# Cross attention: router weights made the stationary operand in four column groups, with a new order of the steps

## The chip, the cores and the metric

The kernel runs on one core of one Trainium2 chip. The metric is the device time of the whole program in microseconds (us), as the median of repeated executions. Four executions of the kernel before took 3863.5, 3868.45, 3855.14 and 3864.93 us; their median is 3864.22 us.

The engines are named as in the profile: PE is the matrix engine (PEld its weight loads), DVE the vector engine, ACT the scalar engine, POOL the GpSimd engine, SP the queue that issues most transfers. PE multiplies a stationary operand, which is loaded into the array first, by a moving operand that streams past it. Results land in PSUM, and another engine has to read them out.

## The reference

The model is one decoder layer in float32 on 32 sequences of 128 tokens with 512 features: differential self attention, cross attention, and a mixture of experts. Cut to what matters here:

```
x = x + self_attention(layernorm(x))
x = x + cross_attention(layernorm(x), ctx)      # 128 channels (the tokens), 8 heads of 16, 512 positions
h = layernorm(x).reshape(4096, 512)
scores = sigmoid(h @ gate_w)                    # gate_w: 512 x 32, the router
# best 2 of 4 groups of experts, then the best 6 experts of those; weights normalized
out = x + experts(h, chosen, weights) + shared_expert(h)
```

The change is about `h @ gate_w`, which is computed for each sequence (128 tokens x 512 features times 512 x 32), and about the order in which all the work of cross attention and of the routing is issued.

## The kernel before

The program has five stages that follow each other: self attention, cross attention with the routing, the first three groups of the shared expert, the routed experts, and the last five groups of the shared expert. The change lies in the second one, `CrossAttention`, and in the few calls to it that run at the end of the first and at the start of the third.

**Steps.** Cross attention handles one sequence ("batch" b) at a time and pipelines them. A batch has 16 steps, two sides of the heads by four chunks of 128 queries by two pairs of heads; batch b begins at step 16 b. In step n, `maxima` (L685) multiplies queries by keys in two row groups of the array (L691) and DVE takes the negated maximum of each row (L695, tile `nm`). Eleven steps later `exponentials` (L708) multiplies the same operands the other way round, with the maxima folded in (L714), and ACT takes the exponential (L718, tile `xp`). The two products of one step use opposite pairs of row groups, so they can run side by side. `weigh` (L721) sums values by these weights for a whole side at once: 16 products in four column groups of 32 (L729), after which DVE transposes the result (L736, tile `xu`).

**Order.** `plan` (L798) lists every other piece of work of a batch with a step, counted from 16 b, and a phase. `advance` (L847) runs through the steps: in each it issues the pieces with phase `first` or `sooner`, then the exponentials, then `middle`, then the maxima, then `after` and `later`. That loop stands under a manual schedule, so PE, DVE, ACT and POOL execute in exactly the order in which the pieces are issued; only SP's queue is ordered by the framework. Since batches overlap, what matters in the steady state is the step modulo 16. We write r0 to r15 for it.

**PSUM.** `Common.banks` (L46) hands out PSUM in turn from four buffers. Each product of any piece takes one; the fifth taker waits until the reader of the first is done. A step takes two.

**The other pieces** and what they issue: `project` (L644; PE L648, ACT L650, POOL L651), `rotate` (L654; DVE L658, four POOL instructions), `measure` and `measure_out` (two ACT passes L73 and L74, three small POOL ones), `normalize` and `normalize_out` (ACT L87), `values` (PE L678, two ACT copies L680), `turn_maxima` (PE L96, DVE L703), `divide` (DVE L746, POOL L748), `turn_out` (DVE L756), `leave` (PE L765, ACT L769, POOL L770, a store), `hand_over` (stores, PE L96, ACT L786), `router` (PE L793, ACT L946, POOL L947), and of the routing `sigmoid` (DVE), `groups` (DVE, POOL), `choose` (DVE, POOL), `take` (DVE L999 and L1004), `count` (PE L1011 and L1012, DVE, POOL L1016), `slots_of` (DVE L1022, POOL) and six times `enter` (POOL, an indirect transfer, L1028).

A float32 product runs as two passes, so a product shows as two records of PE and two weight loads.

Of the kernel before, what the change touches and what calls it, by code (L numbers as in the profile page):

```python
# [10 lines left out]
F32 = mybir.dt.float32  # L11
I32 = mybir.dt.int32
AF = mybir.ActivationFunctionType
ALU = mybir.AluOpType
AX = mybir.AxisListType
# [3 lines left out]
P = 128  # L19
E = 512  # L20
EC = E // P
# [4 lines left out]
NX = 32  # L26
# [73 lines left out]
class Later:  # L100
# [5 lines left out]
    def put(self, step, phase, call, *args):  # L106
        self.calls.append(((step, phase), call, args))
# [420 lines left out]
class CrossAttention:  # L528
# [49 lines left out]
    def prepare(self, heads):  # L578
        nc, wp = self.nc, self.wp
        TC, NH, C = self.TC, self.NH, self.C  # L580

        self.keep = wp.tile([P, 2], F32, name="keep")
        nc.vector.tensor_reduce(self.keep, heads.rearrange("p (j s) -> p s j", s=2), AX.X, ALU.add)
        lane = wp.tile([P, 1], I32, name="lane")
        nc.gpsimd.iota(lane, pattern=[[0, 1]], base=0, channel_multiplier=1)
        nc.vector.tensor_scalar(lane, lane, 31, None, ALU.bitwise_and)
        self.extra = wp.tile([P, 2], F32, name="extra")
        for side in range(2):
            nc.vector.tensor_scalar(
                self.extra[:, side : side + 1], lane, float(self.ROW[side]), None, ALU.is_equal  # L590
            )
        self.zero = wp.tile([P, 1], F32, name="zero")
        nc.vector.memset(self.zero, 0.0)

        self.nm = [[wp.tile([P, TC, P], F32, name=f"nm{s}{i}") for i in range(2)] for s in range(2)]
        self.v2 = [wp.tile([P, TC, NH, 2 * C], F32, name=f"v2{i}") for i in range(2)]
        for t in (*self.nm[0], *self.nm[1]):  # L600
            nc.gpsimd.memset(t, 0.0)
        for t in self.v2:
            nc.gpsimd.memset(t, 1.0)


        self.wT = {}
        for n in "qkvo":
            ps = self.cm.banks()[:, 0, 0:P]
            nc.tensor.transpose(ps, self.nat[n], self.cm.ident)
            self.wT[n] = wp.tile([P, P], F32, name=f"{n}T")  # L610
            nc.vector.tensor_copy(self.wT[n], ps)


        one = wp.tile([P, 1], F32, name="x_one")
        nc.vector.memset(one, 1.0)
        ps = self.cm.banks()[:, 0, 0:1]
        nc.tensor.matmul(ps, self.rotT, one, start=True, stop=True)
        sign = wp.tile([P, 1], F32, name="sign")
        nc.vector.tensor_copy(sign, ps)
        nc.vector.tensor_scalar(self.sin["k"], self.sin["k"], sign, None, ALU.mult)  # L620
        for t, name in ((self.cos, "cosq"), (self.sin, "sinq")):
            t["q"] = wp.tile([P, E], F32, name=name)
            nc.vector.tensor_scalar(t["q"], t["k"], 0.25, None, ALU.mult)


        ps = self.cm.banks()[:, 0, 0:1]
        nc.tensor.matmul(ps, self.wT["o"], self.bv, start=True, stop=True)
        nc.vector.tensor_tensor(self.bo, self.bo, ps, ALU.add)
# [157 lines left out]
        self.nc.scalar.copy(self.out[b], tr)  # L786
        self.nc.sync.dma_start(out=self.h3T_d[b], in_=self.out[b])

    def router(self, b):
        h3T = self.out.pop(b)  # L790
        pl = self.cm.banks()[:, 0, 0:NX]
        for c in range(EC):
            self.nc.tensor.matmul(  # L793
                pl, h3T[:, c, :], self.gw[:, c, :], start=c == 0, stop=c == EC - 1
            )
        self.routing.scores(b, pl)

    def plan(self, load_shared, load_tokens):  # L798

        S, put, routing = self.S, self.todo.put, self.routing  # L800
        first, sooner, middle, after, later = self.PHASES
        for b in range(self.B):
            at = 2 * S * b
            put(at - 20, sooner, self.load, b)
            put(at - 16, sooner, self.project, b, "k")
            put(at - 12, sooner, self.measure, b)
            put(at - 9, sooner, self.rotate, b, "k")
            put(at - 10, sooner, self.normalize, b)
            put(at - 9, sooner, self.project, b, "q")
            put(at - 6, middle, self.rotate, b, "q")  # L810
            put(at + 2, sooner, self.values, b)
            put(at + 9, later, self.turn_maxima, b, 0)
            put(at + 17, later, self.turn_maxima, b, 1)
            put(at + 10, sooner, self.load_again, b)
            put(at + 29, later, self.divide, b)
            put(at + 34, later, self.turn_out, b)
            put(at + 38, later, self.leave, b)
            put(at + 43, later, self.measure_out, b)
            put(at + 48, sooner, self.normalize_out, b)
            put(at + 50, sooner, self.hand_over, b)  # L820
            put(at + 58, sooner, self.router, b)
            put(at + 59, sooner, routing.sigmoid, b)
            put(at + 63, middle, routing.groups, b)
            put(at + 66, middle, routing.choose, b)
            put(at + 66, later, routing.take, b)
            put(at + 70, later, routing.count, b)
            put(at + 80, sooner, routing.slots_of, b)
            for k in range(TOPK):
                put(at + 82 + 5 * k // 2, later, routing.enter, b, k)
            put(at + 19, after, self.weigh, b, 0, 0)  # L830
            put(at + 20, first, self.weigh, b, 0, 1)
            put(at + 28, after, self.weigh, b, 1, 0)
            put(at + 28, later, self.weigh, b, 1, 1)
        put(20, later, load_shared)
        put(2 * S * (self.B - 2), later, load_tokens)
        self.todo.calls.sort(key=lambda x: x[0])
        self.steps = [
            (b, side, c, pair)
            for b in range(self.B) for side in range(2) for c in range(self.TC) for pair in range(2)
        ]  # L840
# [869 lines left out]
```

## Time and profile before

| What | Value |
|---|---|
| Median of four executions | 3864.22 us |
| The profiled execution's own time | 3864.3 us |
| Its span | 3862.6 us, 1.7 us less than its time |
| PE busy | 3776.2 us (98%) |
| DVE, ACT, POOL busy | 53%, 43%, 61% |
| Granted PE clock, mean | 0.993 |
| Cross attention, 798 to 1797 us, PE busy | 971.82 of 999.00 us |
| From one router product to the next in the steady state | 33.05 us (27 times, within 0.01) |

The busy share of PE must be read with care. A record of a product covers its way through the array, and the records of row or column groups that run side by side overlap. PE counts as busy as long as any record is open, also where the next product could have begun earlier. So 98% does not say that PE could not go faster. How long a stretch of work takes is read from the starts of its records, not from the busy share.

### The profile page before, as it was taken

What the parts mean: (1) busy time and instruction counts of PE and PEld (TensorE: products, weight loads), DVE (VectorE), ACT (ScalarE), POOL (GpSimd) and SP (SyncE); (2) the same over time, 40 slices, a digit from 0 to 9 for tenths busy, and PEclk for the clock granted to TensorE, in tenths of its full rate; (3) what the DMA queues carried; (4) which work ended last, traced back from release to release, by engine and by line L of the source; (5) the groups of instructions that cost most, each with busy time, mean ns of one, the idle gap of its engine ahead of it and who ended that gap; (6) DMA issues with size and microseconds to landing.
All of it is one profiled execution on the core that took longest, in us unless ns stands there. A gap on an engine that the chain in (4) does not pass through costs nothing. (4 is left out here: it accounts for less than half of the span.)

```text
span 3862.6 us, 58185 instructions
## 1 busy us (share of the span) xinstructions
PE 3776.2 (98%) x19060; PEld 2010.3 (52%) x19060; DVE 2057.6 (53%) x3202; ACT 1678.3 (43%) x4032; POOL 2349.2 (61%) x2582
## 2 busy tenths in 40 slices
PE   8999999899999999999999999999999999999999
PEld 5666666434444444444445555555555555555444
DVE  5888888777778778777223333333333333333111
ACT  6989998857776777676201111111111111111000
POOL 3545554645777777776337777777777777775000
PEclk9999999899999999999999999999999999999999
DMA  3111110121111111111156777676767777776210
GB/s 111 34 34 37 37 36 26 39 83 50 61 61 50 50 48 47 50 50 34 60 160 165 173 170 169 162 176 153 183 153 166 169 185 154 173 168 155 87 57 33
DMA packets 285988, 387.21 MB, mean 100 GB/s; under 512 B 147889, under 2 KB 179249, under 8 KB 285617
## 3 DMA queue, kind: packets, MB, share of 16 engines
q0 software_dynamic: 62912, 109.85, 15.9%
q1 hardware_dynamic: 81792, 190.98, 15.2%
q10 hardware_dynamic: 140976, 82.60, 7.7%
q8 instruction: 154, 2.52, 0.3%
q14 instruction: 154, 1.25, 0.1%
HBM read 617.52 MB, written 143.07 MB: 197 GB/s over the span
## 5 line engine op out<-in xcount | busy, mean ns | idle before, releaser
L1422 POOL DMA_INDIRECT e_xr<-h_d,e_run_of x832 | 849.1, 1020 | 281.3 <-issue 269.6
L695 DVE TENSOR_REDUCE nm<-ps 128x2 f32<-128x1024 f32 x512 | 610.7, 1215 | 112.4 <-PE ps L691 105.5
L718 ACT ACTIVATE xp<-ps 128x1024 f32<-128x1024 f32 x512 | 505.8, 1021 | 264.9 <-PE ps L691 200.7
L1452 DVE TENSOR_TENSOR e_gu<-e_act,ps 128x352 f32<-128x352 f32 x208 | 108.4, 521 | 942.1 <-ACT e_act L1451 568.3
L1483 PE MATMUL ps<-wd,e_guT 128*128 128x512 f32 (+1 forms) x1248 | 572.8, 595 | 11.3 <-DMA wd<-in_L_ffn_w_down_dram 5.2
L714 PE MATMUL ps<-xqn,xk 32*128 32x512 f32 x2048 | 527.1, 620 | 20.5 <-ACT xp L718 19.1
L1447 PE MATMUL ps<-wg,e_xT 128*128 128x352 f32 x1664 | 528.9, 460 | 4.0 <-DMA wg<-in_L_ffn_w_gate_dram 4.0
L691 PE MATMUL ps<-xk,xq 32*128 32x512 f32 x2048 | 527.4, 630 | 0.5 <-DVE nm L695 0.4
L1447 PE MATMUL ps<-wu,e_xT 128*128 128x352 f32 x1664 | 526.5, 459 | 0.4 <-DMA wu<-in_L_ffn_w_up_dram 0.3
L1451 ACT ACTIVATE e_act<-ps 128x352 f32<-128x352 f32 x208 | 96.3, 463 | 923.1 <-PE ps L1447 426.4
L1447 PEld LDWEIGHTS ps<-wg,e_xT 128*128 128x128 f32 x1664 | 315.3, 190 | 238.9 <-issue 104.3
L1488 POOL DMA_INDIRECT sum_d<-e_y,e_into x208 | 335.9, 1615 | 130.8 <-issue 79.8
L1447 PEld LDWEIGHTS ps<-wu,e_xT 128*128 128x128 f32 x1664 | 316.0, 190 | 177.8 <-DMA wu<-in_L_ffn_w_up_dram 1.5
L279 ACT ACTIVATE s<-s,a_nm 128x128 f32<-128x128 f32 x1024 | 395.5, 394 | 5.3 <-DVE a_nm L265 4.5
L1483 PEld LDWEIGHTS ps<-wd,e_guT 128*128 128x128 f32 (+1 forms) x1248 | 236.6, 191 | 261.2 <-issue 219.3
L714 PEld LDWEIGHTS ps<-xqn,xk 32*128 32x128 f32 x2048 | 168.6, 183 | 284.1 <-ACT xp L718 123.2
L1487 ACT ACTIVATE e_y<-ps,e_weight 128x512 f32<-128x512 f32 x208 | 142.9, 687 | 395.8 <-PE ps L1483 268.6
L1473 DVE STREAM_TRANSPOSE e_guT<-e_gr 96x384 f32<-96x384 f32 (+1 forms) x416 | 230.9, 555 | 60.4 <-DMA e_gr<-e_gu_d 46.1
L228 POOL TENSOR_SCALAR k<-kz,a_keep,a_extra 128x256 f32<-128x256 f32 x128 | 82.4, 653 | 285.9 <-ACT kz L227 285.9
L1028 POOL DMA_INDIRECT table_d<-entry,at x192 | 202.3, 1054 | 64.2 <-issue 53.3
L729 PE MATMUL ps<-xp,v 128*32 128x512 f32 x2048 | 233.0, 595 | 7.9 <-ACT xp L718 7.6
L1434 DVE STREAM_TRANSPOSE e_xT<-e_xr 128x512 f32<-128x512 f32 x208 | 226.4, 1089 | 8.1 <-DMA e_xr<-h_d,e_run_of 8.0
(272 smaller groups left out, 5275.7 us busy)
## 6 DMA issues: line engine op xcount, KB each, us to landing
wg<-in_L_ffn_w_gate_dram SPq DMA_DIRECT2D x208, 704.0 KB
wu<-in_L_ffn_w_up_dram SPq DMA_DIRECT2D x208, 704.0 KB
wd<-in_L_ffn_w_down_dram SPq DMA_DIRECT2D x208, 576.0 KB
e_gu_d<-e_gu ACTq DMA_DIRECT2D x208, 192.0 KB
e_gr<-e_gu_d ACTq DMA_DIRECT2D x208, 192.0 KB
wd<-in_L_ffn_w_down_dram SPq DMA_DIRECT2D x208, 128.0 KB
e_xr<-h_d,e_run_of POOLq DMA_INDIRECT x832
xres<-in_x_dram SPq DMA_DIRECT2D x32, 256.0 KB
```

What stands on the lines that cost most here:

```text
L279: nc.scalar.activation(s[:, j, c, side, :], s[:, j, c, side, :], AF.Exp, bias=nm[n][:, side, at : at + 1], accum_out=sm[n][:, to : to + 1],)
L691: self.nc.tensor.matmul(sc[:, i, :], q[rows, ts(c, P)], k[rows, :], start=True, stop=True)
L695: self.nc.vector.tensor_reduce(at[:, self.ROW[side], 2 * pair : 2 * pair + 2], sc, AX.X, ALU.max, negate=True)
L714: self.nc.tensor.matmul(sc[:, i, :], k[rows, ts(c, P)], q[rows, :], start=True, stop=True)
L718: self.nc.scalar.activation(e, sc, AF.Exp)
L729: self.nc.tensor.matmul(po[b, side][ts(j, 32), :], self.v2[b % 2][:, c, 2 * j + side, :], es[j // 2][:, j % 2, :], start=c == 0, stop=c == ...
L1422: self.cm.nc.gpsimd.indirect_dma_start(out=xr[:, t, :], out_offset=None, in_=self.h3_d.rearrange("t (q f) -> (t q) f", q=self.Q), in_offse ...
L1434: self.cm.nc.vector.transpose(xT.rearrange("p c (t i) -> p c t i", t=self.Q), self.xr.pop(i).rearrange("p t (j c) -> p c t j", c=EC),)
L1447: nc.tensor.matmul(pgu[:, half, 0:M], t[:, c, :], w[:, c, :], start=c == 0, stop=c == EC - 1)
L1473: self.cm.nc.vector.transpose(t[rows, 0:n, :].rearrange("p c (t i) -> p c t i", t=self.Q), g[rows, :, 0 : 32 * n].rearrange("p t (j c) -> ...
L1483: nc.tensor.matmul(py, t[:n, c, :], self.wd[s][:n, c, :], start=c == 0, stop=c == len(M_CHUNKS) - 1)
L1488: nc.gpsimd.indirect_dma_start(out=self.sum_d[:, :], out_offset=bass.IndirectOffsetOnAxis(ap=self.into[:, i : i + 1], axis=0), in_=y[:, :] ...
```

## The change

In `prepare`, a new tile `x_stack` (128 x 32) is made once: four 32 x 32 identities on top of each other. The router is split in two pieces. `logits` multiplies in four column groups: chunk c of the router weights (128 x 32) is the stationary operand of column group c, and the transposed tokens of the same chunk (128 x 128) stream past it. The four partial sums land in 32 rows each of one 128 x 128 PSUM area, and ACT copies that to SBUF (`x_parts`). `router` then multiplies `x_parts` as stationary operand by `x_stack`, which adds the four parts and turns them back to tokens by experts.

All steps and phases in `plan` are new. In the order in which they now come in a period: `hand_over` at r0; `turn_maxima` of side 1 and `values` at r1; `project` k and `measure` at r2; `choose`, `turn_out`, `rotate` k, `take`, `logits` and `normalize` at r3; `weigh` of side 0 at the turn from r3 to r4; `count` at r5; `leave` at r6; `router`, `turn_maxima` of side 0, `project` q, `slots_of`, `measure_out` and `rotate` q at r10; `sigmoid`, `groups` and `normalize_out` at r11; `weigh` of side 1 at the turn from r11 to r12; `load` and `divide` at r14.

```diff
+        self.stack = wp.tile([P, NX], F32, name="x_stack")
+        nc.vector.tensor_reduce(
+            self.stack, self.cm.ident.rearrange("p (c e) -> p e c", e=NX), AX.X, ALU.add
+        )
...
-    def router(self, b):
+    def logits(self, b):
+
         h3T = self.out.pop(b)
-        pl = self.cm.banks()[:, 0, 0:NX]
+        parts = self.cm.banks()[:, 0, 0:P]
         for c in range(EC):
             self.nc.tensor.matmul(
-                pl, h3T[:, c, :], self.gw[:, c, :], start=c == 0, stop=c == EC - 1
-            )
+                parts[ts(c, NX), :], self.gw[:, c, :], h3T[:, c, :], start=True, stop=True
+            )
+        self.out[b] = self.p2.tile([P, P], F32, name="x_parts")
+        self.nc.scalar.copy(self.out[b], parts)
+
+    def router(self, b):
+        pl = self.cm.banks()[:, 0, 0:NX]
+        self.nc.tensor.matmul(pl, self.out.pop(b), self.stack, start=True, stop=True)
         self.routing.scores(b, pl)
...
-            put(at - 20, sooner, self.load, b)
-            put(at - 16, sooner, self.project, b, "k")
-            put(at - 12, sooner, self.measure, b)
-            put(at - 9, sooner, self.rotate, b, "k")
-            put(at - 10, sooner, self.normalize, b)
-            put(at - 9, sooner, self.project, b, "q")
-            put(at - 6, middle, self.rotate, b, "q")
-            put(at + 2, sooner, self.values, b)
-            put(at + 9, later, self.turn_maxima, b, 0)
+            put(at - 18, middle, self.load, b)
+            put(at - 14, sooner, self.project, b, "k")
+            put(at - 14, middle, self.measure, b)
+            put(at - 13, middle, self.rotate, b, "k")
+            put(at - 13, later, self.normalize, b)
+            put(at - 6, sooner, self.project, b, "q")
+            put(at - 6, later, self.rotate, b, "q")
+            put(at + 1, later, self.values, b)
+            put(at + 10, sooner, self.turn_maxima, b, 0)
             put(at + 17, later, self.turn_maxima, b, 1)
-            put(at + 10, sooner, self.load_again, b)
-            put(at + 29, later, self.divide, b)
-            put(at + 34, later, self.turn_out, b)
-            put(at + 38, later, self.leave, b)
-            put(at + 43, later, self.measure_out, b)
-            put(at + 48, sooner, self.normalize_out, b)
-            put(at + 50, sooner, self.hand_over, b)
+            put(at + 26, later, self.load_again, b)
+            put(at + 30, later, self.divide, b)
+            put(at + 35, middle, self.turn_out, b)
+            put(at + 38, sooner, self.leave, b)
+            put(at + 42, later, self.measure_out, b)
+            put(at + 43, later, self.normalize_out, b)
+            put(at + 48, sooner, self.hand_over, b)
+            put(at + 51, later, self.logits, b)
             put(at + 58, sooner, self.router, b)
-            put(at + 59, sooner, routing.sigmoid, b)
-            put(at + 63, middle, routing.groups, b)
-            put(at + 66, middle, routing.choose, b)
-            put(at + 66, later, routing.take, b)
-            put(at + 70, later, routing.count, b)
-            put(at + 80, sooner, routing.slots_of, b)
+            put(at + 59, later, routing.sigmoid, b)
+            put(at + 59, later, routing.groups, b)
+            put(at + 67, middle, routing.choose, b)
+            put(at + 67, later, routing.take, b)
+            put(at + 69, later, routing.count, b)
+            put(at + 74, later, routing.slots_of, b)
             for k in range(TOPK):
-                put(at + 82 + 5 * k // 2, later, routing.enter, b, k)
-            put(at + 19, after, self.weigh, b, 0, 0)
-            put(at + 20, first, self.weigh, b, 0, 1)
-            put(at + 28, after, self.weigh, b, 1, 0)
-            put(at + 28, later, self.weigh, b, 1, 1)
+                put(at + 81 + 5 * k // 2, later, routing.enter, b, k)
+            put(at + 19, later, self.weigh, b, 0, 0)
+            put(at + 20, sooner, self.weigh, b, 0, 1)
+            put(at + 27, later, self.weigh, b, 1, 0)
+            put(at + 28, sooner, self.weigh, b, 1, 1)
```

## The prediction

> **What bounds the kernel now.** I read the page's engine table first, then the stretches by stage, then the chain that ended last, then PE's timeline over one period of cross attention, and last the groups.
>
> ```profile
> PE 3776.2 (98%) x19060; PEld 2010.3 (52%) x19060; DVE 2057.6 (53%) x3202; ACT 1678.3 (43%) x4032; POOL 2349.2 (61%) x2582
> ...
> by line: PE ps L1215 4.5%; PE ps L1247 2.2%; PE ps L1231 0.4%; PE ps L1254 0.3%; DVE s_x L1258 0.0%; issue 0.0%
> ...
> 1208.77:1241.82 33.05, 32.18 (x234) 14.23 (x230) 26.33 (x41) 23.24 (x33) 24.15 (x35) 1.00 0.16 49
> ```
>
> The chain covers only the end (from 3569.85 us) and says nothing of cross attention. The stages run one after another, and the stage of the routed experts (2005 to 3570 us) shows PE busy for 1547.99 of 1565.00 us, so time gained or lost in cross attention should go straight to the end. The last line is one period of cross attention: 33.05 us, with PE, PEld, DVE, ACT and POOL busy for 32.18, 14.23, 26.33, 23.24 and 24.15 us. No engine but PE is near full, and PE's 32.18 hides waits. This is one block of steps in the timeline (start, length, engine, line):
>
> ```profile
> 1208.77 0.70 PE L714 MATMUL ps<-xqn,xk 32*128 32x512 f32 x2
> ...
> 1209.74 1.02 PE L714 MATMUL ps<-xqn,xk 32*128 32x512 f32 x4
> ...
> 1209.94 1.94 ACT L718 ACTIVATE xp<-ps 128x1024 f32<-128x1024 f32 x2 [2.43 <-PE ps L691]
> 1210.00 3.68 DVE L695 TENSOR_REDUCE nm<-ps 128x2 f32<-128x1024 f32 x3 [0.38 <-PE ps L691]
> ...
> 1211.02 0.70 PE L714 MATMUL ps<-xqn,xk 32*128 32x512 f32 x2 [0.21 <-ACT xp L718]
> ...
> 1211.28 0.70 PE L691 MATMUL ps<-xk,xq 32*128 32x512 f32 x2
> ...
> 1212.34 0.41 PE L1011 MATMUL ps<-taken,before 128*128 128x32 f32 x2
> ```
>
> Steps begin at 1208.77 and 1209.74, so a free step takes 0.97 us. The third begins only at 1211.02: it needs the PSUM buffer of the first exponentials, which ACT frees at 1209.94 + 1.02 = 1210.96. Its maxima start at 1211.28, after DVE's first reduction (1210.00 + 1.23). The ring of four buffers is what binds. From this: a block of two steps costs 2.25 us (the next piece also waits for the first exponential), a block of three costs 3.57 (1212.34 - 1208.77).
>
> ```profile
> 1218.27 0.66 PE L96 MATMUL ps<-ident,nm 128*128 128x128 f32 x4
> 1218.77 0.98 PE L793 MATMUL ps<-gw,h3T 128*128 128x32 f32 x8
> 1219.67 0.70 PE L714 MATMUL ps<-xqn,xk 32*128 32x512 f32 x2
> ...
> 1223.54 3.64 PE L729 MATMUL ps<-xp,v 128*32 128x512 f32 x32
> 1227.11 0.70 PE L714 MATMUL ps<-xqn,xk 32*128 32x512 f32 x2
> ```
>
> The router takes 0.90 us (1218.77 to 1219.67). The 32 passes of `weigh` take 3.57, 0.11 each, while a full-array pass of 512 columns takes 0.43 (3.43 for the eight of L1215): four column groups do run side by side.
>
> ```profile
> L695 DVE TENSOR_REDUCE nm<-ps 128x2 f32<-128x1024 f32 x16 | 19.1, 1215 | 3.6 <-PE ps L691 3.4
> L718 ACT ACTIVATE xp<-ps 128x1024 f32<-128x1024 f32 x16 | 15.8, 1021 | 7.8 <-PE ps L691 6.1 <-PE ps L714 1.7
> ```
>
> These two free the ring; each waits for PE, and PE for them, in turn.
>
> **The period before, by starts on PE.** From r4: three steps 3.57; count, leave, project q 0.47 + 0.94 + 0.95; r7-r9 3.57; turn_maxima 0.50, router 0.90; r10-r12 3.87 (0.30 over: DVE does turn_maxima 0.68 and the q shuffle 0.73 before the reduction); weigh 3.57; r13-r15 3.58; project k 1.05; r0-r1 2.26; turn_maxima, hand_over, values 2.00; r2-r3 2.25; weigh 3.57. Sum 33.05.
>
> **The router on PE.** Removed: 0.90. Added: the last product, two passes with 32 moving columns; L1011 has that shape and takes 0.24 (1212.34 to 1212.58). Added: `logits`, eight passes of 128 columns in four groups. Lower bound, perfect overlap: 2 x 0.11 = 0.22. Upper bound, none: `values`, eight such passes on the full array, takes 1.07 (1234.93 to 1236.00). I take 0.35, near the lower end, because `weigh` is the nearest row: its two-pass ideal plus the 0.13 that it needs above its own ideal (3.57 - 8 x 0.43). Net -0.31 a batch.
>
> **The added copy and buffer.** ACT's copies take 0.375 us for 256 columns and 0.585 for 512, so 128 columns are about 0.27. ACT has 9.8 us idle in the period. The copy comes after the exponentials of r3, beside `weigh`, which keeps PE for 3.57 us. It also frees a buffer that is wanted again four takers later, by the exponentials of r5; by my walk it ends 2.4 us earlier than that. Without the cover it would cost at most 0.27. The page TensorEngine Tiling (Array Packing) of the Trainium skill warns, under PSUM Bottleneck, that column tiling speeds up PE but not the reading of PSUM, which may become the bound. Were the copy wholly on the path, the period below would be 0.27 longer and the total 8 us more. The same page says under Key Properties that a change of tiling mode drains PE; the row for it is a first pass that takes 0.53 us instead of 0.43, and since `logits` stands beside `weigh`, in the same mode, no change of mode is added.
>
> **The new order.** Blocks of 3, 3, 3, 3, 2, 2 steps between other PE work become 2 (r4), 4 (r6), 2 (r10), 4 (r12), 2 (r0), 2 (r2). A block of four, from the rows above: third step at 2.25 and 2.51, the fourth's exponentials when those row groups are through (3.48), its maxima when DVE's second reduction ends (3.64), out 1.05 later: 4.69. So 2 + 4 costs 6.94 where 3 + 3 costs 7.14.
>
> The walk from r4, each start being the latest of PE's queue, the buffer, and the reader's own queue: r4-r5 2.25; count and leave 1.41; r6-r9 4.68; router and turn_maxima 0.76 (the second waits 0.02 for a reduction); project q 0.95 after 0.15 of waiting for the exponentials of r9; r10-r11 2.24; weigh 3.57; r12-r15 4.69; hand_over 0.45; r0-r1 2.42 (the reduction of r15 is 0.34 late behind `divide`'s reciprocal); turn_maxima, values, project k 2.65; r2-r3 2.25; logits 0.35; weigh 3.57. Sum 32.39, so -0.66: -0.31 by the router, -0.57 by the blocks (19.10 to 18.53), +0.22 of small new waits (0.17 ahead of PE products, 0.05 around hand_over and values).
>
> What the moves put in front of other work, queue by queue. DVE at r3: choose 0.7, turn_out 0.7 and the k shuffle 0.73 now stand ahead of one reduction, take 0.85 behind it. The reduction ends 0.45 us before the maxima of r4 need its buffer, because logits and weigh (3.92) run meanwhile. DVE at r10-r11: slots, the q shuffle, sigmoid and groups (0.34 + 0.73 + 0.54 + 0.4) lie beside the other weigh. ACT: measure (1.56) delays the exponentials of r3 and measure_out those of r11, both read only after a weigh. POOL: the q rotation (4.2 us in four instructions) now waits behind measure_out's three small ones, which wait for ACT; it ends some 3 us before the first maxima at r0 need it, as before. Indirect transfers stay six, on POOL. SP: x1 is now asked for after its buffer is free instead of 6 steps before (`load_again` waited up to 14.2 us in SP's queue), and nothing on SP is needed within a period; worth nothing.
>
> **From period to total.** Router to router is 33.05 us 27 times, and some four further batches have a large part of the period: 29 x 0.66 = 19.1. Four last batches run beside the shared expert and save only the 0.31 on PE: some 0.4 beyond what is counted. The entry (720 to 800 us), where PE falls to half clock in four windows (0.70 and 0.76 granted in 720-740 and 740-760), issues the same work in other places: 0 taken, bounds -8 and +8, since one window of 10.24 us at half clock costs up to 5.1. `x_stack` is one DVE reduction, under 1.2 us once, beside self attention: 0. From the profiled execution: 3864.3 - 19.5 = 3844.8; it stands 0.1 above the median, so 3845. Its own range, with the period between 32.1 and 32.6 and the entry's bounds partly used: 3832 to 3854.
>
> **Rivals.**
>
> *The router's gain fails, the rest is filled by waits.* If column groups with separate products of 128 columns do not overlap, logits costs 1.07 instead of 0.35, the period becomes 33.1, and the time 3864 or so; with half of the overlap it is 32.75, 3855. For it: 128 columns are short against a weight load (0.109 for 32 columns, eight of them). Against it: `weigh` issues its four groups 0.01 us apart.
>
> *Slower: DVE's pile at r3.* The 2.13 us of DVE work ahead of the reduction of r3 have 0.45 us of slack by my walk. If DVE reaches it later, PE stands after weigh, in every period. Lateness up to 0.45 costs nothing, 1.11 uses up the gain, and from 1.5 the kernel is slower by 0.3%; all 2.13 on the path would give 32.39 + 2.13 - 0.45 = 34.07, +30 us, 3894. For it: it is the thinnest slack in the order, and ACT's measure stands in the same place. Against it: every input of that work is ready 3 us or more ahead.
>
> *Nothing changes.* The period could be held by something I do not see, with PE only waiting elsewhere. Against it: no other engine is busy beyond 26.33 of 33.05. It would give 3860 to 3866.
>
> **How the numbers follow.** Forecast 0.62; router or waits eat it, or nothing changes, 0.21; slower 0.17. About 0.3% (11.6 us) is what a measurement of this kernel can tell from no change. Faster 0.61, same 0.22, slower 0.17. The range takes in the gain with a short entry below and reaches into the slow case above: 3828 to 3872.
>
> **What would show it.** After: router to router at 32.4 us; logits about 0.35 and router 0.24 between starts; blocks of four steps at 4.7; no PE wait on DVE after weigh. The prediction is wrong if PE waits for `nm` at r4, or if logits takes near 1 us, or if the stages after 1843 us become longer.

## The result, and the profile after

| | Before | After |
|---|---|---|
| Median of the executions, us | 3865.73 (68) | 3869.34 (45) |
| Ratio, 95% interval | | 1.0011, 1.0006 to 1.0017 |
| Profiled execution: own time, span, us | 3864.3, 3862.6 | 3876.94, 3875.0 |
| Period of cross attention, us | 33.05 | 33.31 (25 times), 32.53 (twice) |

The change makes the kernel slower by some 4 us (2.3 to 6.6 by the interval), less than the 0.3% that the prediction takes as the least that a measurement of this kernel can tell. The forecast was a gain of 19.5 us. The profiled execution lies 7.6 us above its own median, so the two spans must not be subtracted; the periods can be.

This is one period of the kernel after (a stretch of the timeline: its bounds and length, then the busy time of PE, PEld, DVE, ACT and POOL, the granted clock, the share and rate of the transfers):

```profile
1202.59:1235.90 33.31, 32.34 (x241) 13.57 (x233) 27.28 (x42) 23.72 (x35) 24.21 (x35) 1.00 0.16 49
```

Beside the line of before, PE is busy 0.16 us more, ACT 0.48 (0.26 of it is the new copy), POOL 0.06 and DVE 0.95. DVE was given no new work in the period; so something on it became longer. The starts on PE give the place:

| Stretch of the period | Forecast, us | After, us | Without the collision (below), us |
|---|---|---|---|
| r4-r5 | 2.25 | **3.03** | 2.25 |
| count, leave | 1.41 | 1.50 | 1.50 |
| r6-r9 | 4.68 | 4.70 | 4.71 |
| router, turn_maxima, project q | 1.86 | 2.06 | 2.06 |
| r10-r11 | 2.24 | 2.25 | 2.25 |
| weigh | 3.57 | 3.57 | 3.57 |
| r12-r15 | 4.69 | 4.71 | 4.70 |
| hand_over | 0.45 | 0.58 | 0.59 |
| r0-r1 | 2.42 | 2.34 | 2.34 |
| turn_maxima, values, project k | 2.65 | 2.48 | 2.48 |
| r2-r3 | 2.25 | 2.25 | 2.25 |
| logits | 0.35 | 0.27 | 0.26 |
| weigh | 3.57 | 3.57 | 3.57 |
| Sum | 32.39 | 33.31 | 32.53 |

Of the 0.92 us between forecast and result, 0.78 are the block r4-r5. Its timeline (start, length, engine, line; in brackets the idle time before it and what ended it):

```profile
1238.75 1.27 POOL L663 TENSOR_TENSOR rot<-rot,sin 128x512 f32<-128x512 f32 x1
1238.80 1.44 DVE L1011 TENSOR_TENSOR hits<-number,picked 128x192 f32<-128x192 f32 x1
...
1239.47 0.70 PE L718 MATMUL ps<-xqn,xk 32*128 32x512 f32 x2
...
1240.27 0.49 DVE L1016 TENSOR_REDUCE taken<-hits 128x32 f32<-128x192 f32 x1
...
1240.68 0.71 DVE L740 STREAM_TRANSPOSE xu<-ps 128x512 f32<-128x512 f32 x1
...
1241.44 0.30 PEld L695 LDWEIGHTS ps<-xk,xq 32*128 32x128 f32 x4 [0.80 <-DVE xu L740]
1241.44 1.13 PE L695 MATMUL ps<-xk,xq 32*128 32x512 f32 x4
...
1242.50 0.41 PE L1023 MATMUL ps<-taken,before 128*128 128x32 f32 x2
```

Read it from the bottom. `count` (L1023) can't start before 1242.50, because the maxima of r5 started only at 1241.44. They waited for DVE's transpose of what `weigh` had left (`xu`, L740), which frees their PSUM buffer. The transpose stood in DVE's queue behind the reduction of `take` (L1016), and that behind the comparison of `take` (L1011), which took 1.44 us. These are the durations of that comparison over all batches (minimum, median, maximum in ns; the one line that shows it, after and before):

```profile
L1011 DVE TENSOR_TENSOR hits<-number,picked x32: 316/1442/1460, 905.7 to 1919.9; 128x192 f32<-128x192 f32 x32
```

```profile
L999 DVE TENSOR_TENSOR hits<-number,picked x32: 348/349/365, 907.8 to 1921.1; 128x192 f32<-128x192 f32 x32
```

The same instruction on the same shapes takes four times as long in 25 of the 32 batches. In each of these 25, POOL's product of the rotation of k (L663, 1.27 us) had begun 0.04 to 0.05 us before, and the comparison ended 0.2 us after it. In batch 24 the comparison was first by as little, and POOL's product was the longer one instead:

```profile
1704.39 0.35 DVE L1011 TENSOR_TENSOR hits<-number,picked 128x192 f32<-128x192 f32 x1
1704.44 1.44 POOL L663 TENSOR_TENSOR rot<-rot,sin 128x512 f32<-128x512 f32 x1
```

Behind that batch, and behind batch 20, where POOL came 0.37 us later, lie the two periods of 32.53. The last five batches, with no rotation left beside them, took 0.32 to 0.36. Before, the rotation of k ran in another part of the period (r7), and `take` ran in 23 of the 32 batches beside an indirect transfer that POOL was issuing; it still took 0.35:

```profile
1237.56 1.09 POOL L1028 DMA_INDIRECT table_d<-entry,at  x1 [0.16 <-POOL entry L990]
...
1238.38 0.35 DVE L999 TENSOR_TENSOR hits<-number,picked 128x192 f32<-128x192 f32 x1
```

The Trainium skill has the rule for this, on the page SBUF — State Buffer, sections "SBUF: two separate sides" and "Who interferes with whom": DVE and GpSimd share one pair of ports to SBUF; a DVE instruction whose two inputs both lie in SBUF contends there with a GpSimd instruction that reads SBUF, and whichever starts first holds the pair for its whole length. No run here shows what a POOL instruction does that only writes SBUF. The rows agree with the rule: both sizes of the pair (1.44 and 0.35, 0.35 and 1.44) and the order that decides; and beside the indirect transfer nothing became longer. They don't show that the ports are the reason; that is the page's statement. The one that was held ended sooner after the other (0.21 us, and 1.13 in batch 24) than it takes alone (0.35 and 1.27), by 0.14 us both times. DVE's one-input instructions beside the same POOL work were not longer: L1016 took 0.49 beside L664, and 0.50 before.

### The profile page after: what moved, and what is told of

The parts are those of the page before. It is cut to its first block, busy times and chain, and to the rows that moved or that the text cites. A ratio compares the mean times of both kernels' runs of the same rounds, so it can differ in the third digit from the quotient of the medians.

```text
span 3875.0 us, 58345 instructions
## 1 busy us (share of the span) xinstructions
PE 3775.6 (97%) x19124; PEld 1993.5 (51%) x19124; DVE 2080.9 (54%) x3203; ACT 1693.8 (44%) x4064; POOL 2350.6 (61%) x2582
```

## The experiments

The experiments ran on three chips; every ratio is to the kernel before, run on the same chip (3855.62 us on the first, 3910.97 and 3910.77 for the other two sets), so only ratios and periods, not times, can be compared between sets. Periods come from the profile of each kernel.

| Kernel | Router | Collision | Period, us | Ratio, 95% interval |
|---|---|---|---|---|
| After | new | yes | 33.31 | 1.0011, 1.0006 to 1.0017 |
| enter_before_turn | new | no | 32.53 | 0.9948, 0.9934 to 0.9961 |
| enter_before_turn_dve_longer | new | no, DVE delayed | 33.32 | 1.0026, 1.0017 to 1.0035 |
| old_router_new_order | old | yes | 33.59 | 1.0012, 1.0003 to 1.0021 |
| new_router_old_order | new | no | 32.85 | 0.9994, 0.9985 to 1.0003 |
| old_router_no_collision | old | no | 32.55 | 0.9953, 0.9936 to 0.9969 |
| old_router_no_collision_again | old | no | 32.55 | 0.9964, 0.9951 to 0.9976 |
| enter_before_turn_again | new | no | 32.54 | 0.9970, 0.9955 to 0.9985 |
| enter_before_turn_third | new | no | 32.53 | 0.9962, 0.9947 to 0.9977 |

### Is it the collision?

Theory A: DVE's `take` collides with POOL's rotation. Rival: something else of the new order holds r5. The first kernel takes away what collides. The shuffle on DVE stays where it is; the four POOL instructions of the rotation of k move a step back, so that the indirect transfer that POOL issues at the end of r3 comes first and `take` runs beside that, as before.

```diff
-            put(at - 13, middle, self.rotate, b, "k")
+            put(at - 13, middle, self.shuffle, b, "k")
+            put(at - 12, sooner, self.turn, b, "k")
```

> The changed kernel with one swap on POOL: the four POOL instructions of the k rotation are issued at the start of step 4 mod 16, behind the indirect transfer of `enter`, instead of ahead of it. DVE's queue, PE's and ACT's stay as they are. Theory A (DVE's comparison in `take`, which reads two SBUF tiles, is held for 1.1 us by the POOL multiply of the rotation that starts 0.04 us before it): the comparison falls from 1.44 to 0.35 us in all batches, the period from 33.31 to 32.53 us, and the time from 3869 to about 3849 us (26 periods by 0.78). Theory B (the pile of DVE work at step 3 is simply too long): DVE's work is unchanged, so the period stays at 33.3 us and the time at 3869, within 3 us.

Measured: period 32.53, ratio 0.9948, so about 20 us faster than the kernel before. The two later sets with this kernel gave 0.9970 and 0.9962, some 12 to 15 us; 26 periods that are 0.52 us shorter make 13.5. Only the first batch still collides (`take` 1.45, the period behind it 33.32). This is the place of the collision now:

```profile
1198.91 0.34 DVE L1020 TENSOR_TENSOR hits<-number,picked 128x192 f32<-128x192 f32 x1
1199.07 1.16 POOL L1049 DMA_INDIRECT table_d<-entry,at  x1 [0.18 <-issue]
1199.28 0.48 DVE L1025 TENSOR_REDUCE taken<-hits 128x32 f32<-128x192 f32 x1
...
1199.71 0.72 DVE L748 STREAM_TRANSPOSE xu<-ps 128x512 f32<-128x512 f32 x1
...
1200.26 1.28 POOL L671 TENSOR_TENSOR rot<-rot,sin 128x512 f32<-128x512 f32 x1
```

`take` takes 0.34 us, the transpose starts 0.80 us after it instead of 1.88, and the block r4-r5 is 2.25, as forecast. POOL's rotation now runs beside DVE instructions that read PSUM; they keep their 0.72 and 1.2 us.

The second kernel leaves the order mended and gives DVE the lost time back, as two reductions behind `take` whose results are not used. If only DVE's lateness counts, the period must return.

```diff
+        for n in (512, 304):
+            nc.vector.tensor_reduce(self.spare, self.long[:, 0:n], AX.X, ALU.max)
```

> The kernel with the swap on POOL, plus two reductions of 512 and 304 elements on DVE right behind `take` (about 1.1 us, one SBUF input each, results not used). It puts back on DVE the time that the wait took, without any wait for POOL. Theory A: only the lateness of DVE counts, so the period is back at about 33.3 us and the time at about 3869 us. If POOL itself were what holds the period, it would stay at 32.5 and 3849.

Measured: period 33.32, ratio 1.0026, `take` 0.36. The two reductions take 1.18 us, and PE shows the same wait of 0.8 us for the transpose:

```profile
1241.61 0.36 DVE L1022 TENSOR_TENSOR hits<-number,picked 128x192 f32<-128x192 f32 x1
...
1242.01 0.48 DVE L1027 TENSOR_REDUCE taken<-hits 128x32 f32<-128x192 f32 x1
...
1242.41 1.18 DVE L1029 TENSOR_REDUCE spare<-cos 128x1 f32<-128x512 f32 x2
...
1244.27 0.30 PEld L704 LDWEIGHTS ps<-xk,xq 32*128 32x128 f32 x4 [0.81 <-DVE xu L749]
```

So DVE's lateness alone is enough for the whole loss in the period, and 1.1 us of it cost 0.8 us a period: 0.3 us were free.

### What are the router and the order worth?

Two kernels do one half of the change each.

```diff
# old_router_new_order: the changed kernel with the router of before
-            put(at + 51, later, self.logits, b)
# new_router_old_order: the kernel before with the new router
+            put(at + 51, after, self.logits, b)
```

> The changed kernel with the old router in one piece at step 58 (no logits, no copy, no stacked identities): the new order alone. Theory A: the comparison in `take` still takes 1.44 us, and since DVE is what is late from step 2 to step 5, taking logits (0.27) away there gains nothing, while the router at step 10 costs 0.90 instead of 0.35 on PE: period about 33.8 us, time 3880 to 3886 us. If the new router were what makes the kernel slower, this one would be at or below 3866 us.

> The kernel before with the new router alone: logits at step 51 ahead of weigh, the product with the stacked identities at step 58; everything else in the old order. Theory A: PE does 0.27 + 0.24 instead of 0.90, no two-input comparison meets POOL, so the period falls from 33.05 to about 32.7 us and the time from 3866 to about 3855 us. Rival (the new router costs time through its copy and its PSUM buffer): 3866 us or more.

Measured: 33.59 and 32.85. Both miss. The new order with the old router collides as well (`take` 1.45 in 25 of the 27 batches that have a rotation beside them), at 33.59 instead of 33.8. It was expected 14 to 20 us above the kernel before (3866 us) and lies some 5 us above it on its own chip. The two batches without the collision have 32.55. The new router in the old order was expected to save 0.35 us a period and saves 0.20: the router's 0.90 became 0.44 for the last product, from its start to the next, and 0.26 for `logits`. Its time can't be told from that of before. The third kernel has both remedies: old router, new order, no collision.

> The new order with the router of before, in one piece at r10, and with the rotation of k behind the entries on POOL, as in enter_before_turn. It tells what the router alone is worth when nothing else disturbs the period. If the router saves what it saved in the other two pairs (0.28 us a period between old_router_new_order and the changed kernel, 0.20 between the kernel before and new_router_old_order), the period is 32.73 to 32.81 us here, against 32.53 with the new router. If the router's time is hidden in this order, as the two undisturbed periods of old_router_new_order say (32.55), the period is 32.55. In the stage of the shared expert (from the last weigh to the first expert product) three profiles with the new router and new order gave 188.2 to 188.9 us, one with the new router and the old order 186.6, and the two with the old router 183.0 and 183.4. Theory room (the new tile x_parts pushes the shared expert's tiles s_x2, s_gu and s_act up by 1024 bytes a partition, and that slows the transfer of the experts' weights): no x_parts here, so 183 to 184. Theory router (the new router's work itself, which ends otherwise beside the shared expert): 183 to 184 too. Theory chance (the stage varies from execution to execution): anything from 183 to 189. Time from that, with 3855.6 us before: 3832 to 3841.

Measured: 32.55. So without the collision the whole gain of 0.50 us comes from the order, and the router adds 0.02. PE's starts around the old router, then around the new one, both without the collision:

```profile
1208.67 1.08 PE L805 MATMUL ps<-gw,h3T 128*128 128x32 f32 x8
1209.59 0.64 PE L96 MATMUL ps<-ident,nm 128*128 128x128 f32 x4
1210.06 1.02 PE L652 MATMUL ps<-h,qT 128*128 128x512 f32 x2
1211.01 0.70 PE L726 MATMUL ps<-xqn,xk 32*128 32x512 f32 x2
```

```profile
1208.03 0.41 PE L814 MATMUL ps<-x_stack,x_parts 128*128 128x32 f32 x2
...
1208.38 0.66 PE L96 MATMUL ps<-ident,nm 128*128 128x128 f32 x4
...
1209.03 0.30 PEld L652 LDWEIGHTS ps<-h,qT 128*128 128x128 f32 x2 [0.24 <-ACT xp L730]
1209.03 1.13 PE L652 MATMUL ps<-h,qT 128*128 128x512 f32 x2
...
1210.09 0.70 PE L726 MATMUL ps<-xqn,xk 32*128 32x512 f32 x2
```

The old router lasts 0.92 to the next start, the new product 0.35. But turn_maxima then lasts 0.65 to the next start instead of 0.47, since project q behind it now waits for the exponentials of r9 (ACT L730), a wait that does not show behind the old router. Project q itself lasts 1.06 instead of 0.95; why is not shown. The three together take 2.34 and 2.06, so 0.28 is left; `logits`, before `weigh`, costs 0.26. That is the 0.02. With the collision the router was worth 0.28, because there `logits` fills a wait that is on PE anyway: without it r4-r5 takes 3.30 us instead of 3.03, and PE waits 1.07 us for `xu` instead of 0.80.

### The stage of the shared expert

From the last `weigh` to the first product of the routed experts, the profile before has 183.0 us and that after 188.2. Here PE waits 3.81 us for DVE's `s_gu`, which stands behind DVE's transpose of the first gathered tokens (before, then after):

```profile
2006.07 1.10 DVE L1434 STREAM_TRANSPOSE e_xT<-e_xr 128x512 f32<-128x512 f32 x1 [5.85 <-DMA e_xr<-h_d,e_run_of]
```

```profile
2007.64 1.10 DVE L1446 STREAM_TRANSPOSE e_xT<-e_xr 128x512 f32<-128x512 f32 x1 [8.61 <-DMA e_xr<-h_d,e_run_of]
...
2013.52 2.38 PE L1266 MATMUL ps<-sd,s_gu 64*128 64x512 f32 x4 [3.81 <-DVE s_gu L1251]
```

DVE waits 2.8 us longer for the gathers. They are issued at the same point, 24.6 us after the first transfer of the experts' weights. These share the transfer engines with them and arrive more slowly: 31 us after the first was issued, 8.60 MB of the first four experts' 8.65 were there before, 8.00 after. First theory, "room": the tile `x_parts` moves the shared expert's tiles by 1024 bytes. Two kernels exchange the layouts: old router with two unused tiles of that size, and new router with `x_parts` in the place of `h3`.

```diff
# old_router_room_of_parts
+        for i in range(2):
+            self.nc.vector.memset(p2.tile([P, P], F32, name="x_parts"), 0.0)
# parts_in_h3
-        self.out[b] = self.p2.tile([P, P], F32, name="x_parts")
+        self.out[b] = self.h3.pop(b)[:, 0:P]
```

> As old_router_no_collision, but two tiles of the size of x_parts are set to zero once and never used, so that the shared expert's tiles lie where they lie in the changed kernel, 1024 bytes higher, while the router is the old one. Theory room: the shared stage takes 188 to 189 us and the total is 5 us above old_router_no_collision. Theory router: 183 to 184 us and no difference. Theory chance: anything from 183 to 189. The period is that of old_router_no_collision in every theory.

> As enter_before_turn, but x_parts takes the place of h3 of the same batch, which nothing reads any more, instead of a tile of its own; so the shared expert's tiles lie where they lie in the kernel before, while the router is the new one. Period 32.53 us in every theory. Theory room: the shared stage takes 183 to 184 us, and the total is 5 us below enter_before_turn: 3832 to 3833, ratio 0.9935. Theory router: 188 to 189 us, 3838. Theory chance: anything from 183 to 189.

> The same kernel as enter_before_turn, for a second profile of it and a time on the same chip as the other three. Period 32.53 us. Theories room and router: the shared stage takes 188 to 189 us again, and 3838 us in all. Theory chance: the stage may come out between 183 and 189, and the total no different from parts_in_h3.

Measured: 183.5 and 189.8 us, the opposite of what "room" says; the ratios are 0.9950 and 0.9961. That speaks against it twice. But these are single profiles, and the stage varies by itself: old_router_no_collision, with the old router, had 188.4 in one profile and 184.0 in another. enter_before_turn_again had 189.4. The second theory, "fetch", came from the list of transfers: of those on the instruction queues one, of 16 KB, comes for about every 250 records of PE and PEld, and the new router has 128 more records. The last four runs put 32 small unused products at the start of PE's program, where PE waits for data.

```diff
+        ps = self.banks()
+        for i in range(32):
+            nc.tensor.matmul(
+                ps[0:32, 0, 0:32], self.ident[:, 0:32], self.ident[:, 0:32], start=True, stop=True
+            )
```

> As old_router_no_collision (old router, new order, rotation behind the entries), with 32 small products (32 x 32, two passes each, unread) put at PE's very start, where PE otherwise waits 12 us for its first data. They are 128 records of PE, as many as the new router adds over the 32 batches. Seen so far: the traces hold one transfer of 16 KB on an instruction queue for every 256 records of PE; with the new router one of them falls 0.8 to 2.7 us after the first transfer of the experts' weights begins, with the old router none until 30 us, and in all ten profiles the weights arrive later with the new router. Theory fetch (that transfer, falling among the first of the weights, sets them back): the shared stage goes to 188 to 190 us, the fetch stands at 1 to 3 us, and the total is about 5 us above old_router_no_collision. Theory router (something else of the new router does it): 183 to 185 us, no difference. Periods 32.55 us in both.

> As enter_before_turn, with the same 32 small products at PE's start: with the 128 records of the new router that makes 256, a whole block, so the fetch falls again where it fell with the old router, at 30 us. Theory fetch: the shared stage goes back to 183 to 185 us and the total is about 5 us below enter_before_turn. Theory router: 188 to 190 us, no difference. Periods 32.53 us in both.

> The same kernel as old_router_no_collision, beside the other three on one chip. Fetch theory and router theory: shared stage 183 to 185 us; a second 188 would say that this stage varies by itself. Period 32.55 us, ratio to the kernel before 0.995.

> The same kernel as enter_before_turn, beside the other three on one chip. Fetch theory and router theory: shared stage 188 to 190 us. Period 32.53 us, ratio to the kernel before 0.995 to 0.997.

These are the transfers in 10 us that begin 1.1 us before the first weight transfer is issued, with the old router, without and with the 32 products (queue, kind: packets, MB, share of 16 engines):

```profile
q1 hardware_dynamic: 388, 2.01, 63.2%
q0 software_dynamic: 174, 0.50, 22.2%
q14 instruction: 1, 0.01, 0.2%
```

```profile
q1 hardware_dynamic: 396, 2.03, 64.4%
q0 software_dynamic: 180, 0.51, 19.7%
q8 instruction: 1, 0.02, 1.2%
q14 instruction: 1, 0.01, 0.2%
```

| Kernel | Router | 16 KB fetch, us after the first weight transfer was issued | Shared stage, us |
|---|---|---|---|
| before; old_router_new_order | old | 30.1; 30.2 | 183.0; 183.4 |
| old_router_no_collision; again | old | 30.4; 30.4 | 188.4; 184.0 |
| old_router_room_of_parts | old | 30.6 | 183.5 |
| old_router_128_more | old | 1.1 | 188.8 |
| new_router_128_more | new | 29.7 | 188.7 |
| new_router_old_order | new | 0.8 | 186.6 |
| after; dve_longer; parts_in_h3 | new | 2.7; 4.0; 1.8 | 188.2; 188.8; 189.8 |
| enter_before_turn; again; third | new | 2.0; 1.7; 1.7 | 188.9; 189.4; 189.1 |

The products moved the fetch as expected both times, to 1.1 and to 29.7 us. The stage followed once (184 to 188.8 with the old router) and not the other time (188.7 with the new one). All eight profiles with an early fetch have 186.6 us or more, four of the six with a late one 183.0 to 184.0. So the new router isn't needed for the longer stage, and the fetch alone doesn't explain it. The times don't settle it either: old_router_128_more had a ratio of 0.9971 (0.9959 to 0.9984), new_router_128_more 0.9950 (0.9933 to 0.9968), with nearly the same stage. What makes the weights arrive more slowly stays open.

## Why the prediction was wrong

**The step that failed** is "DVE at r3", and in it "take 0.85 behind it". `take` was priced by a row of before where no rotation ran beside it, and the walk had put `rotate` k and `take` in the same step on two engines without asking what one does to the other. It cost 1.88 us from its start to the transpose behind it instead of 0.80, and r4-r5 took 3.03 us instead of 2.25. The slower rival named this pile of DVE work and gave a price: lateness beyond 0.45 us goes to the period, 1.11 uses up the gain. The lateness was 1.08 and the period 33.31, 0.92 above the forecast one. That rival's mechanism, DVE late after `weigh`, is what happened, but one step further on (the maxima of r5, which wait for `xu`, not those of r4, which wait for `nm`), and for a reason that its case did not hold. "Every input of that work is ready 3 us or more ahead" held for choose and turn_out (6.2 and 4.2 us) and nearly for the k shuffle (2.9), not for `take`, whose `picked` POOL had written 0.42 us before. That didn't cost anything, since DVE came to `take` straight from the reduction of r3; it had its inputs and was slow.

**The router, -0.31.** `logits` came out better than priced (0.27 for 0.35). The gain was lost at r10: 0.17 us of new waits ahead of PE products had been forecast; the last product, turn_maxima and project q together stand 0.40 above what they take elsewhere (2.06 less 0.24, 0.47 and 0.95). Net 0.02 instead of a gain of 0.14 after the forecast waits. This is the rival "the router's gain fails, the rest is filled by waits" by its second half; its first half, no overlap of the column groups, is excluded by 0.27 against 1.07. The first pass of 0.53 us that the prediction takes as the row for a change of tiling mode doesn't show one: the same 0.53 stands in its own rows behind a mere wait, with no change of mode (1211.02, the next start at 1211.55).

**The blocks, -0.57.** Right but for r4-r5 with the collision. A block of four took 4.70 and 4.71 for 4.68 and 4.69, blocks of two 2.25 and 2.34 for 2.25 and 2.42. Without the collision the period is 32.53 for 32.39; the 0.14 are turn_maxima and project q (0.20), hand_over (0.13) and leave (0.09), less what r0-r1, project k and logits saved.

**The copy at nothing.** Right: `x_parts` takes 0.26 us beside `weigh`, and nothing waits for it.

**From period to total.** "Time gained or lost in cross attention should go straight to the end" held for the periods: the stretch from the first `weigh` to the last is 1028.0 us before, 1029.5 after, 1010.8 to 1011.7 without the collision. From the periods alone the stretch after would be 5.5 us longer (25 by 0.26, less 2 by 0.52); the first and last batches gave 4 us back. The entry, taken as 0, gave 2.5 us (811.7 us to the first `weigh` before, 809.2 after, 808.8 to 811.0 in all kernels of the new order). What lay outside every case is the shared stage; the prediction only names longer stages after 1843 us as a sign that it is wrong. Its 5 us make up the rest of the loss of 4 us if they hold in the median too, which the runs don't prove. The two stages behind it, whose code is unchanged, are 8.2 us longer in the profile after, about what that execution lies above its median.

## What to carry to other kernels

When a step is moved, list for each new neighbour on DVE and POOL not only when it is ready but what it reads: a DVE instruction with two SBUF operands beside a POOL instruction that reads SBUF can take as long as the POOL one, and 0.04 us decide which of the two is held. An instruction that is longer after a change although its shape is the same is found fastest by its minimum, median and maximum over the batches. And PE time saved in front of pieces that a ring of buffers holds is not yet time saved: here 0.57 us less in one product left 0.28 us, and the other half of the split took that.

## What the runs showed of the hardware

- A comparison of 128 x 192 on DVE with two SBUF operands took 0.35 us alone or beside an indirect transfer issued by POOL, and 1.43 to 1.46 us when a 1.27 us product of POOL had started up to 0.05 us before. Started 0.05 us ahead, it took 0.35 and the product 1.44.
- Eight float32 passes of 128 columns in four column groups took 0.26 to 0.27 us between starts on PE, where eight on the full array took 1.07.
- A transfer of 16 KB on an instruction queue came for about every 250 records of PE and PEld, 154 to 156 in the program. 128 more records, half of that, moved it from 30 us to 1 us after the first weight transfer was issued.
- The best kernel found, enter_before_turn, is the changed one with four POOL instructions moved by one step: 0.9948, 0.9970 and 0.9962 of the time before in three sets of runs. The same order with the old router is as good: 0.9953 and 0.9964.
